# Eight layers on one core: Mamba and the last layer become tasks of the planner that already orders the first six

## The chip, the cores and the metric

The kernel runs on one core of a Trainium2 chip. The time is device microseconds of one execution, from the first to the last instruction and what the device adds around them. Engines: PE multiplies matrices (PEld is its loading of weights), DVE, ACT and POOL work element by element, SP issues the transfers between DRAM and SBUF. PE writes its results to PSUM, which holds eight banks of 512 floats a partition.

## The reference

The input x has 8 sequences of 256 tokens with 128 features, in float32. Eight layers follow each other, and each is used in the same way:

```python
x = x + _layernorm(layer(_layernorm(x)))
```

The layers are a gated delta rule, a block of local attention with a feed-forward part, a line-based attention, a ternary feed-forward network, an attention in tiles, a mixture of experts with two of eight experts, a Mamba pair and a quantized feed-forward network. The change is about the last two. The Mamba layer runs one scan forwards and one over the flipped sequence:

```python
xn = _layernorm(x, ln1_w, ln1_b)
# for each direction m, with E = 256 channels and N = 64 states:
xp, z = split(xn @ W_in.T)
xc = silu(causal_conv4(xp) + conv_b)
dt_lo, Bm, Cm = split(xc @ W_xp.T)           # 8, 64, 64
dt = softplus(dt_lo @ W_dt.T + dt_b);  A = -exp(A_log)
h[t] = exp(dt[t] * A) * h[t-1] + (dt[t] * xc[t]) * Bm[t]     # 256 x 64 values
y[t] = sum_n h[t][:, n] * Cm[t][n] + xc[t] * Dp
out_m = (y * silu(z)) @ W_out.T
# and together:
layer = _layernorm(out_1 + flip(out_2), ln2_w, ln2_b) + xn
```

The last layer is `(silu(x @ wg.T) * (x @ wu.T)) @ wd.T` with 384 hidden features and weights that are integers divided by 127.

## The kernel before

All tokens live in one SBUF tile `k.x`, 16 blocks of 128 tokens. A group g is 4 blocks, 512 tokens, two sequences.

**The first six layers** are written as tasks. A task is a Python generator with a rank (the order in which it was added), a list of tasks that have to be finished before it, and steps divided by `yield`. The class `Turns` is a planner that runs while the program is built: it keeps a clock for each engine, durations for each kind of instruction, and three classes of slots ("ps": four PSUM buffers of two banks each; "4k" and "2k": 25 SBUF buffers of each size). `run` picks the step that can start first, and among equals the one of lowest rank, and emits its instructions. `as_written` then ties each compute engine's queue to the order in which they were emitted, so the engines execute each queue strictly in that order. `S.ps()` hands out a PSUM buffer and writes filler products ahead of a step where the planner expects PE to be idle for over 1.5 us (line 351). A string such as `yield "4k+5"` asks for a slot, and for five more to be free. `change` is a task after the first layer that gives its weights' space to the weights of the last two layers.

**The Mamba layer** stands behind all that, in pools of its own and written out by hand. A unit u is a group and a direction m; there are eight, with 64 states each. `prologue(u)` makes the norms, the convolution, the gate `sz`, the step sizes `dt`, the inputs `dtxT` and the matrices B and C; `epilogue(u)` turns the sum back, adds `D * xc`, multiplies the gate, multiplies by W_out, and for the second direction adds both, takes norms and adds to `k.x`. One state n of a unit is a chain over all engines:

- SP loads one row of C to all partitions (`Cs`, L2046); for even n ACT scales `dtxT` by a column of B (`sT`, L2050); ACT makes `dA` by two exponentials (L2053).
- PE writes the state's input into PSUM: eight transposes of `sT` for even n (L2068), 32 products of 64x64 with the block matrix `dB` for odd n (L2066). POOL makes `dB` for four states at a time (L2040).
- DVE runs the recurrence over 1024 elements (L2074).
- POOL multiplies h by C to `hc` (L2076); for every eighth state DVE does.
- PE adds `hc`, transposed, into the unit's sum `ps_y` in PSUM (L2086).

The loop goes over states: at turn i it writes the inputs of state i-1, starts state i, scans state i-1 and adds state i-4, and then takes one step of the epilogue of the unit before (`behind`) and one of the prologue of the next (`ahead`). PSUM holds three buffers for inputs and everything else and one for `ps_y`.

A layernorm is statistics on DVE (L227, L228), reciprocal roots by powers on POOL (L230, L231), a factor on DVE (L234) and four activations on ACT (L237).

**The last layer** comes behind the Mamba layer: norms of all 16 blocks, and then four blocks of 512 tokens with products for gate and up (L2156, L2157), silu (L2159), product (L2160), the product with wd (L2164) and the norm. Its norms take a square root on ACT (L204), whose table is loaded each time. At last `k.x` is written out (L2221).

Of the kernel before, what the change touches and what calls it, by code (L numbers as in the profile page):

```python
# [17 lines left out]
P = 128  # L18
NB = 8
# [7 lines left out]
UNITS = 4  # L27

# [8 lines left out]
ON_V = 8  # L37

# [134 lines left out]
class Ctx:  # L173
# [46 lines left out]
    def norm_steps(self, dst, src, n):  # L220
# [9 lines left out]
        nc.gpsimd.tensor_scalar(rs, mv[:, :, 1], EPS, None, ALU.add)  # L230
# [54 lines left out]
class Turns:  # L285
# [7 lines left out]
    def __init__(self, k, es, slots):  # L293
        self.nc, self.k = k.nc, k
        self.pools = {
            c: es.enter_context(k.tc.tile_pool(name="turns_" + c, bufs=n, **({"space": PSUM} if c == "ps" else {"side": "right"})))
            for c, n in slots.items()
        }
        self.slots = {c: [0.0] * n for c, n in slots.items()}
        self.clock, self.starts, self.users = {}, {}, {}  # L300
        self.tables = self.mode = None
        self.tiles = {}
        self.tasks = []
        self.now = self.queue = 0.0
        self.filling = False

    def add(self, name, after, steps):
        self.tasks.append((len(self.tasks), list(after), name, steps))
# [15 lines left out]

    def leaving(self, *classes):
        self.leave(*classes)
        return
        yield
# [8 lines left out]
    def adder(self, layer):  # L337
        return lambda name, after, steps: self.add((layer, *name), after, steps)
# [77 lines left out]
    def run(self):  # L416
# [4 lines left out]
        while live or todo:  # L421
            for task in [t for t in todo if all(a in ends for a in t[1])]:
                todo.remove(task)
                order, after, name, steps = task
                live.append([order, max([ends[a] for a in after], default=0.0), {}, name, steps, 0])
            best = None
            for task in live:
                order, ready, needs, _, steps, at = task
                if any(len(self.slots[c]) < n + spare for c, (n, spare) in needs.items()):
# [7 lines left out]
                key = (max(ready, free), order)  # L437
# [1398 lines left out]
def load_l3_attn(k, pool):  # L1836
    k.flip = k.load("c_flip", [P, P], pool)
    k.l3a_ln = k.load("l3a_ln", [P, 4, D], pool, bcast=True)
    k.l3a = []
    for m in ("m1", "m2"):  # L1840
# [3 lines left out]
        k.nc.sync.dma_start(out=w["wdt"][64:73], in_=k.I[f"l3a_{m}_wdt"])  # L1844
        k.l3a.append(w)


def l3_attn(k):

# [12 lines left out]
    N = 64  # L1864
    HALF = (slice(0, 64), slice(64, 128))
    with ExitStack() as es:
        s1 = es.enter_context(k.tc.tile_pool(name="l3a_s1", bufs=1))
        s2 = es.enter_context(k.tc.tile_pool(name="l3a_s2", bufs=2))
        s3 = es.enter_context(k.tc.tile_pool(name="l3a_s3", bufs=3))
        dram = es.enter_context(k.tc.tile_pool(name="l3a_d", bufs=2, space=bass.MemoryType.DRAM))  # L1870
        psum = es.enter_context(k.tc.tile_pool(name="l3a_ps", bufs=3, space=PSUM))
        psumy = es.enter_context(k.tc.tile_pool(name="l3a_psy", bufs=1, space=PSUM))

        def pb(name="ps_a"):
            return psum.tile([P, 2, U], F32, name=name, tag="b")

        for m, w in enumerate(k.l3a):


            w["wk"] = s1.tile([P, 4, 256], F32, name="wk", bufs=2)  # L1880
            cv = s2.tile([P, 4, 256], F32, name="cv", tag="sp_u")
            nc.sync.dma_start(out=cv, in_=k.I[f"l3a_m{m + 1}_conv"].partition_broadcast(P))
            nc.vector.tensor_tensor(w["wk"], cv, over(w["win"][:, 0:256], 4, 1), ALU.mult)
            w["A"] = s1.tile([P, 2, N], F32, name="A", bufs=2)
            nc.scalar.activation(w["A"], w["alog"], AF.Exp)
            nc.vector.tensor_scalar(w["A"], w["A"], 1e-20, -1.0, ALU.max, ALU.mult)
        xTs, CLs = [], []
        for j in range(2):
            t = s1.tile([P, 2, 3 + L], F32, name=f"xT{j}")
            nc.gpsimd.memset(t[:, :, 0:3], 0.0)  # L1890
            xTs.append(t)
            t = s1.tile([P, U], F32, name=f"CL{j}")
            nc.gpsimd.memset(t[64:73, :], 1.0)
            CLs.append(t)
        xns, x1s = {}, {}
        ident64 = k.load("c_ident64", [P, 64], s1)

        def by_seq(t):
            return t.rearrange("p (b t) -> p b t", t=L)

        def turned(name, src):

            t = s2.tile(list(src.shape), F32, name=name)
            for b in range(2):
                for j in range(2):
                    nc.sync.dma_start(out=t[HALF[b], j::2], in_=src[HALF[j], 2 * b:2 * b + 2])
            return t

        def prologue(u, o):
            g, m = divmod(u, 2)  # L1910
            w = k.l3a[m]
            if m == 0:
                xs = xns[g] = s2.tile([P, 4, D], F32, name="xn")
                yield from k.norm_steps(xs, k.x[:, 4 * g:4 * g + 4, :], 4)
                yield from k.norm_steps(xs, xs, 4)
                nc.gpsimd.tensor_tensor(xs, xs, over(k.l3a_ln[:, 0, :], 4, 1), ALU.mult)
                nc.gpsimd.tensor_tensor(xs, xs, over(k.l3a_ln[:, 1, :], 4, 1), ALU.add)
                yield
            xT, CL = xTs[u % 2], CLs[u % 2]
            ps = pb()  # L1920
            for j in range(4):
                d = slice(j * P, (j + 1) * P)
                if m == 0:
                    nc.tensor.transpose(ps[:, 0, d], xns[g][:, j, :], k.ident)
                else:
                    nc.tensor.matmul(ps[:, 0, d], xns[g][:, j ^ 1, :], k.flip, start=True, stop=True)
            yield
            nc.scalar.copy(xT[:, :, 3:3 + L], by_seq(ps[:, 0, :]))
            yield

            xz = s2.tile([P, 4, U], F32, name="xz")
            xc, sz = xz[:, 0:2, :], xz[:, 2:4, :]
            for ec in range(2):
                for b in range(2):
                    ps = pb()
                    for tap in range(4):
                        nc.tensor.matmul(ps[:, 0, 0:L], w["wk"][:, tap, ec * P:(ec + 1) * P], xT[:, b, tap:tap + L], start=tap == 0, stop=tap == 3)
                    yield
                    nc.scalar.activation(xc[:, ec, b * L:(b + 1) * L], ps[:, 0, 0:L], AF.Identity, bias=w["cols"][:, ec, 0:1])
                    yield  # L1940
                    yield
            for ec in range(2):
                ps = pb()
                nc.tensor.matmul(ps[:, 0, :], w["win"][:, 256 + ec * P:256 + (ec + 1) * P], xT[:, :, 3:3 + L], start=True, stop=True)
                yield
                nc.scalar.copy(sz[:, ec, :], ps[:, 0, :])
            yield
            nc.scalar.activation(xz, xz, AF.Silu)
            yield

            ps = pb()
            for ec in range(2):
                nc.tensor.matmul(ps[0:72, 0, :], w["wxp"][:, ec, 64:136], xc[:, ec, :], start=ec == 0, stop=ec == 1)
            for j in range(4):
                for ec in range(2):
                    nc.tensor.matmul(ps[:, 1, j * 64:(j + 1) * 64], xc[:, ec, j * P:(j + 1) * P], w["wxp"][:, ec, 0:64], start=ec == 0, stop=ec == 1)
            yield
            B = s2.tile([P, 4, N], F32, name="B")
            nc.scalar.copy(CL[0:72, :], ps[0:72, 0, :])
            nc.scalar.copy(B.rearrange("p j n -> p (j n)"), ps[:, 1, 0:256])  # L1960
            cd = dram.tile([N, U], F32, name="cd")
            nc.sync.dma_start(out=cd, in_=CL[0:64, :])
            Bt = turned("Bt", B)
            yield
            ps = pb()
            for ec in range(2):
                nc.tensor.matmul(ps[:, ec, :], w["wdt"][64:73, ec * P:(ec + 1) * P], CL[64:73, :], start=True, stop=True)
            dt = s2.tile([P, 2, U], F32, name="dt")
            yield
            nc.scalar.activation(dt, ps, AF.Softplus)  # L1970
            yield
            dtx = s1.tile([P, 2, U], F32, name="dtx")
            nc.gpsimd.tensor_tensor(dtx, dt, xc, ALU.mult)

            nc.gpsimd.memset(dt.rearrange("p e (b t) -> p e b t", t=L)[:, :, :, 0:1], 1e23)
            yield
            yield
            dtxT = s2.tile([P, 4, 2, P], F32, name="dtxT")
            ps = pb()
# [260 lines left out]
```

## Time and profile before

| what | us |
|---|---|
| median of 3 runs | 4137.35 |
| lowest and highest | 4134.76, 4147.18 |
| the profiled execution | 4149.48 |
| its span, first to last instruction | 4147.5 |
| PE, DVE, POOL, ACT busy | 3595.0, 3016.8, 2643.5, 2525.7 |
| first scan of Mamba starts | 2712.3 |
| last scan of Mamba starts | 4059.15 |

A line of the groups gives the code line, engine, operation, what it writes and reads, how often, then busy time and mean duration in ns, then the idle time of the engine ahead of it and what ended most of that. Two rows of the page divide the span into 40 slices and give the busy share of an engine, or the clock granted to PE, in tenths. In a timeline a line is start, duration, engine, code line, operation and tiles, with the idle time ahead of it and its releaser in brackets.

### The profile page before, as it was taken

What the parts mean: (1) busy time and instruction counts of PE and PEld (TensorE: products, weight loads), DVE (VectorE), ACT (ScalarE), POOL (GpSimd) and SP (SyncE); (2) the same over time, 40 slices, a digit from 0 to 9 for tenths busy, and PEclk for the clock granted to TensorE, in tenths of its full rate; (3) what the DMA queues carried; (4) which work ended last, traced back from release to release, by engine and by line L of the source; (5) the groups of instructions that cost most, each with busy time, mean ns of one, the idle gap of its engine ahead of it and who ended that gap; (6) DMA issues with size and microseconds to landing.
All of it is one profiled execution on the core that took longest, in us unless ns stands there. A gap on an engine that the chain in (4) does not pass through costs nothing. (4 is left out here: it accounts for less than half of the span.)

```text
span 4147.5 us, 125166 instructions
## 1 busy us (share of the span) xinstructions
PE 3595.0 (87%) x55265; PEld 2821.2 (68%) x55265; DVE 3016.8 (73%) x4217; ACT 2525.7 (61%) x4465; POOL 2643.5 (64%) x1991
## 2 busy tenths in 40 slices
PE   6989988998888888999899998688988987898886
PEld 4877767777776566655565555377777876777774
DVE  7677677786755666644565568379989987998995
ACT  4555454545444554545354444289979988998993
POOL 5668567666854444331233333479989988998993
PEclk8999999999999999998999898789999999999997
DMA  1000000000001000000000000033323333343430
GB/s 58 3 3 2 3 2 3 3 2 9 2 19 38 1 1 12 25 16 6 1 1 1 6 1 1 11 99 118 111 83 114 109 107 88 110 111 89 118 114 26
DMA packets 98677, 168.89 MB, mean 41 GB/s; under 512 B 16699, under 2 KB 26582, under 8 KB 98006
## 3 DMA queue, kind: packets, MB, share of 16 engines
q1 hardware_dynamic: 98134, 160.89, 13.3%
q8 instruction: 434, 7.11, 0.7%
q14 instruction: 109, 0.89, 0.1%
HBM read 153.51 MB, written 2.10 MB: 38 GB/s over the span
## 5 line engine op out<-in xcount | busy, mean ns | idle before, releaser
L2076 POOL TENSOR_TENSOR hc<-h,Cs 128x1024 f32<-128x1024 f32 x448 | 1049.5, 2372 | 97.1 <-DVE h L2074 85.3
L2074 DVE TENSOR_TENSOR_SCAN h<-dA,ps_h 128x1024 f32<-128x1024 f32 x448 | 988.9, 2266 | 89.8 <-PE ps_h L2068 53.7
L2053 ACT ACTIVATE dA<-dt,A 128x512 f32<-128x512 f32 x1024 | 684.4, 714 | 125.3 <-DVE h L2074 92.6
L2086 PE MATMUL ps_y<-w_c_ident,hc 128*128 128x128 f32 x4096 | 562.1, 281 | 118.7 <-POOL hc L2076 85.3
L2086 PEld LDWEIGHTS ps_y<-w_c_ident,hc 128*128 128x128 f32 x4096 | 454.2, 143 | 173.6 <-POOL hc L2076 158.2
L2050 ACT ACTIVATE sT<-dtxT,B 128x256 f32<-128x256 f32 x1024 | 449.7, 495 | 3.9 <-PE ps_h L2068 3.9
L590 DVE SCALAR_TENSOR_TENSOR acc<-ps,w_l0a_conv,acc 128x254 f32<-128x254 f32 (+2 forms) x768 | 309.5, 471 | 30.6 <-ACT acc L584 30.4
L2066 PE MATMUL ps_h<-dB,dtxTt 64*64 64x64 f32 x16384 | 301.1, 222 | 19.2 <-DVE h L2074 10.1
L2066 PEld LDWEIGHTS ps_h<-dB,dtxTt 64*64 64x64 f32 x16384 | 265.5, 136 | 72.9 <-issue 46.7
L2068 PE MATMUL ps_h<-w_c_ident,sT 128*128 128x128 f32 x2048 | 276.5, 279 | 19.4 <-DVE h L2074 16.9
L2068 PEld LDWEIGHTS ps_h<-w_c_ident,sT 128*128 128x128 f32 x2048 | 239.5, 145 | 31.5 <-DVE h L2074 23.8
L742 POOL TENSOR_TENSOR Ps<-M,w_c_levels 128x512 f32<-128x512 f32 x192 | 241.8, 1274 | 4.8 <-DVE M L716 4.2
L359 ACT COPY XY<-ps 128x1024 f32<-128x1024 f32 (+1 forms) x128 | 120.5, 945 | 179.1 <-PE ps L807 167.1
L230 POOL TENSOR_SCALAR ln_rs<-ln_mv 128x4 f32<-128x4 f32 (+1 forms) x84 | 22.0, 263 | 297.0 <-DVE ln_mv L228 270.5
L800 PE MATMUL ps<-Z,XY 64*64 64x64 f32 x4608 | 172.7, 226 | 35.7 <-DVE Z L784 25.4
L800 PEld LDWEIGHTS ps<-Z,XY 64*64 64x64 f32 x4608 | 144.4, 137 | 53.8 <-DVE Z L784 27.1
L807 PE MATMUL ps<-XY,Z 64*64 64x64 f32 x5120 | 172.0, 224 | 5.2 <-issue 5.1
L784 DVE TENSOR_TENSOR Z<-ps,w_c_ident 128x512 f32<-128x512 f32 x160 | 108.1, 685 | 73.1 <-PE ps L781 71.4
L1633 ACT ACTIVATE e<-ps,nm 128x256 f32<-128x256 f32 x256 | 99.8, 484 | 98.9 <-DVE nm L1630 83.4
L351 PE MATMUL ps<-ident 128*128 128x512 bf16 x401 | 110.0, 426 | 55.2 <-DVE qn L1077 11.5
L2074 DVE TENSOR_TENSOR_SCAN ps_h<-dA,ps_h 128x1024 f32<-128x1024 f32 x64 | 145.6, 2274 | 14.8 <-PE ps_h L2066 14.5
L807 PEld LDWEIGHTS ps<-XY,Z 64*64 64x64 f32 x5120 | 151.1, 138 | 6.9 <-issue 6.9
(451 smaller groups left out, 8572.7 us busy)
## 6 DMA issues: line engine op xcount, KB each, us to landing
Cs<-cd SPq DMA_DIRECT2D x512, 256.0 KB, 3.3
dtxTt<-dtxT SPq DMA_DIRECT2D x32, 128.0 KB, 3.9
wk<-in_l0a_w SPq DMA_DIRECT2D x8, 256.0 KB, 5.7
w_h<-in_l1f_h SPq DMA_DIRECT2D x4, 512.0 KB, 3.9
w_l2a<-in_l2a_w SPq DMA_DIRECT2D x3, 512.0 KB, 4.1
w_l0a_wg<-in_l0a_wg SPq DMA_DIRECT2D x1, 1024.0 KB
w_qk<-in_l0f_wqkv SPq DMA_DIRECT2D x2, 512.0 KB, 3.9
cv<-in_l3a_m_conv SPq DMA_DIRECT2D x2, 512.0 KB, 5.0
```

Of the source, the lines that this page charges most:

```text
L359: self.nc.scalar.copy(out, in_)
L590: nc.vector.scalar_tensor_tensor(acc[:, n, s:L], p4[:, n, 0:L - s], conv[:, h2, 4 * j + n, 3 - s:4 - s], acc[:, n, s:L], ALU.mult, ALU.add,)
L742: nc.gpsimd.tensor_tensor(t, M[:, :, 0:64], over(k.l0a_levels[:, n, :], 8, 1), ALU.mult)
L800: nc.tensor.matmul(ps[own, a, at(j)], XY[rows, t, at(i)], Z[rows, za, at(zj)], start=True, stop=True)
L807: nc.tensor.matmul(ps[to, a, at(4 + j)], Z[rows, za, at(zj)], XY[rows, t, at(i)], start=True, stop=True)
L2050: nc.scalar.mul(st["s"][:, j], o["dtxT"][:, j], o["B"][:, j, n:n + 1])
L2053: nc.scalar.activation(dA[:, :, ec, :], by_seq(o["dt"][:, ec, :]), AF.Exp, scale=w["A"][:, ec, n:n + 1])
L2066: nc.tensor.matmul(ps[q, b, ec, j * 64:(j + 1) * 64], o["dtxTt"][rows, j, ec, q], dB[rows, j, :], start=True, stop=True)
L2068: nc.tensor.transpose(ps[:, j // 2, ec, j % 2 * P:(j % 2 + 1) * P], st["s"][:, j, ec, :], k.ident)
L2074: nc.vector.tensor_tensor_scan(h.rearrange(flat), st["dA"].rearrange(flat), st["in"].rearrange(flat), 0.0, ALU.mult, ALU.add)
L2076: (nc.vector if on_v else nc.gpsimd).tensor_tensor(st["hc"], h, over(by_seq(st["C"]), 2, 2), ALU.mult)
L2086: nc.tensor.matmul(o["py"][:, 2 * b + j, ec, :], st["hc"][:, b, ec, j * P:(j + 1) * P], k.ident, start=first, stop=n == N - 1, is_transpos ...
```

## The change

Mamba and the last layer become tasks of the same planner, so all eight layers share one order, four PSUM buffers and the two classes of SBUF slots.

- Each state of Mamba is a task. It may start when the states eight and nine before it are done (`STATES`). A class of slots "in", without a pool, lets at most two inputs wait in PSUM or be scanned at once. The sum `y` of a unit takes one of the four PSUM buffers; the next unit's is opened when ten states are left.
- The prologue is divided into tasks for the norm, the transposes, the gate and the rest. The gate `sz` and the convolved `xc` are written to DRAM and brought back twelve states before the unit's end (`aside`, `back`). Gate and convolution each have their own silu; the convolution's four parts go into one PSUM buffer.
- The two norms in a row at Mamba's start become one, with a changed epsilon (`twice`).
- The convolution weights folded with W_in and the exponential of `A_log` are made when the weights arrive, during the second layer.
- The last layer is four tasks of 512 tokens, each after the group's second Mamba epilogue. Its norms are those of the planner, without the square root on ACT.
- Tasks may have a rank of their own and a pace that adds to it with each step; Mamba's early tasks leave six slots of each size free while earlier layers still run (`late`, `reserve`).
- `ON_V` is set to 16, but no line uses it any longer: every eighth state still has its product on DVE.

```diff
+STATES, PACE = 8, 1.5
...
-    def norm_steps(self, dst, src, n):
+    def norm_steps(self, dst, src, n, twice=False):
...
+        if twice:
+            nc.gpsimd.tensor_scalar(rs, mv[:, :, 1], 1.0 + EPS, EPS * EPS, ALU.mult, ALU.add)
+        else:
+            nc.gpsimd.tensor_scalar(rs, mv[:, :, 1], EPS, None, ALU.add)
...
+    def more(self, t):
+        self.clock[self.engine] += t
+        self.now = max(self.now, self.clock[self.engine])
...
-                order, ready, needs, _, steps, at = task
-                if any(len(self.slots[c]) < n + spare for c, (n, spare) in needs.items()):
+                order, ready, needs, _, steps, at, pace = task
+                more = self.reserve if order >= self.late > lowest else {}
+                if any(len(self.slots[c]) < n + spare + more.get(c, 0) for c, (n, spare) in needs.items()):
...
-                key = (max(ready, free), order)
+                key = (max(ready, free), order + pace * at)
...
+    def aside(o, name, t):
+        o[name] = k.l3a_dram.tile([P, 2, U], F32, name=name)
+        S.fetch(o[name], t)
+        S.leave("4k")
...
+    def back(u):
+        o = made[u]
+        yield "4k+2 4k"
+        for name in ("xc", "sz"):
+            t = S.tile("4k", [P, 2, U], name)
+            S.fetch(t, o[name])
+            o[name] = t
...
+    def state(u, n):
...
+        on_v = n % 8 == 7
+        yield "2k 4k+1" if n % 2 else "2k 4k+1 4k"
+        C = S.tile("2k", [P, U], "Cs")
...
+        yield "ps in"
+        ps = S.ps().rearrange("p b (e t) -> p b e t", e=2)
...
+        yield "4k" if n % 2 and not on_v else ""
+        h = ps if on_v else S.tile("4k", [P, 2, 2, L], "h")
+        nc.vector.tensor_tensor_scan(h.rearrange(flat), dA.rearrange(flat), ps.rearrange(flat), 0.0, ALU.mult, ALU.add)
+        S.more(1010)
+        if not on_v:
+            S.leave("ps", "in")
+        yield
+        hc = S.tile("4k", [P, 2, 2, L], "hc")
+        (nc.vector if on_v else nc.gpsimd).tensor_tensor(hc, h, over(by_seq(C), 2, 2), ALU.mult)
...
+        add(("r", u), [own("s", u, N - 12), own("z", u)], back(u), rank + N - 12, 1)
+        add(("e", u), [own("r", u)] + [own("s", u, n) for n in range(N)] + [own("e", u - 1)] * m, epilogue(u), rank + N, 2)
+        for n in range(N):
+            i = u * N + n
+            after = [own("s", *divmod(j, N)) for j in (i - STATES, i - STATES - 1) if j >= 0]
...
+            add(("s", u, n), [own("y", u)] + after, state(u, n), rank + n)
...
+    add(("w",), list(soon), weights())
+    for g in H4:
+        add(("f", g), [own("w")] + before(g), forward(g))
...
-            S = Turns(k, es2, {"ps": 4, "4k": N4K, "2k": N2K})
+            S = Turns(k, es2, {"ps": 4, "4k": N4K, "2k": N2K, "in": 2})
...
-            for layer in IN_TURNS:
+            for layer in [l0_attn, l0_ffn, l1_attn, l1_ffn, l2_attn, l2_ffn, l3_attn, l3_ffn]:
...
-        for layer in (l3_attn, l3_ffn):
-            if layer in layers:
-                layer(k)
```

## The prediction

> **What bounds the kernel now.** I read the page first, then the engine table by stretches, then the waits and the timeline at the places that the change touches.
>
> ```profile
> span 4147.5 us, 125166 instructions
> PE 3595.0 (87%) x55265; PEld 2821.2 (68%) x55265; DVE 3016.8 (73%) x4217; ACT 2525.7 (61%) x4465; POOL 2643.5 (64%) x1991
> DVE  7677677786755666644565568379989987998995
> PEclk8999999999999999998999898789999999999997
> ```
>
> PE leads over the span, but the slices disagree: from slice 28 on DVE stands at 8 to 9 with a few 7s, and the slices at either end of that stretch (26 and 40) fall to 3 and 5. The first six layers end near 2660 us, the Mamba layer runs its 512 scans from 2712 to 4061, the last layer takes the rest.
>
> ```profile
> L2076 POOL TENSOR_TENSOR hc<-h,Cs 128x1024 f32<-128x1024 f32 x448 | 1049.5, 2372 | 97.1 <-DVE h L2074 85.3
> L2074 DVE TENSOR_TENSOR_SCAN h<-dA,ps_h 128x1024 f32<-128x1024 f32 x448 | 988.9, 2266 | 89.8 <-PE ps_h L2068 53.7
> 2640.00:2712.00 72.00, 37.31 (x108) 22.34 (x108) 17.12 (x63) 25.04 (x46) 30.64 (x36) 0.64 0.14 42
> 3061.00:3099.00 38.00, 26.47 (x391) 23.36 (x389) 24.38 (x40) 21.96 (x46) 27.16 (x19) 0.87 0.16 53
> 3148.00:3223.00 75.00, 65.57 (x1422) 58.03 (x1424) 74.86 (x37) 68.86 (x130) 73.82 (x37) 1.00 0.40 122
> 4061.00:4147.00 86.00, 49.02 (x212) 32.97 (x210) 35.79 (x143) 28.09 (x43) 16.50 (x14) 0.73 0.04 13
> ```
>
> The last four lines are stretches: length, then busy PE, PE loads, DVE, ACT, POOL. At a steady pace (3148 to 3223) DVE is busy 74.86 of 75 us: 32 scans and 4 multiplications, 18.7 us for eight states. That is the bound. Between two units (3061 to 3099) DVE is busy 24 of 38 us, and ahead of the first scan and behind the last every engine is half idle.
>
> ```profile
> DVE ln_mv L234 <- POOL ln_rs L231: 12.2, 4, 3.7
> DVE ln_st L227 <- POOL x L2028: 4.4, 1, 4.4
> 2636.42 0.19 DVE L1761 TENSOR_TENSOR p<-p,best 128x32 f32<-128x32 f32 x1
> 2712.27 2.29 DVE L2074 TENSOR_TENSOR_SCAN h<-dA,ps_h 128x1024 f32<-128x1024 f32 x1 [35.81 <-PE ps_h L2068]
> 4059.15 2.27 DVE L2074 TENSOR_TENSOR_SCAN ps_h<-dA,ps_h 128x1024 f32<-128x1024 f32 x1
> 4092.02 1.26 POOL L2033 TENSOR_TENSOR x<-x,yn 128x512 f32<-128x512 f32 x1 [2.02 <-DVE ln_st L214]
> 4141.49 0.40 SPq L2221 DMA_DIRECT2D out<-x  x1
> ```
>
> The first two lines are waits of DVE from 3037 to 3126: layernorm steps stand in DVE's queue in front of scans and wait for POOL. The rest mark the last routing of the sixth layer, the first and last scan, the last add of Mamba, the output.
>
> So the time has three parts here: first scan at 2712.3 (P), first to last scan start 1346.9 (W), last scan start to end 88.4 (T).
>
> **P, the start.** In the queues of the changed kernel the first two scans stand on DVE directly behind the subtraction of the last group's routing, which ran at 2636.4. What is added ahead of that place: on PE the first unit's prologue (16 convolution products of 128x256, 2 of the gate, 2 each of the two projections, 16 transposes and small products; by the 0.86 us between 128x512 products about 13 us), on ACT about 16 us (three table switches there and back at 1.28, 1.0 to 2.0 us for each of gate, convolution, softplus and copies), on POOL 2.5 for the norm, 2.3 for dtx, 3.3 for three dB. PE was busy 83 of 100 us from 2500 to 2600, so I let 8 of its 13 us show; ACT was busy 47 of 100 there, its 16 us are covered. The early layers are the same up to the place where the Mamba weights arrive, then reshuffled in the second layer; DVE gains two multiplications of 1.23 for the folded convolution and 0.5 for A, and loses 0.9 for the last layer's weights. Their loads were issued at 1283 to 1291 and first used at 1355, so nobody waits; without that cover it is some 10 us. A reshuffle can cost or win: bounds -10 and +15. P = 2636.4 + 8 + 1 = 2645, from 2630 to 2665.
>
> **W, the scans.** What each engine has to do between first and last scan, counted in the changed queues. DVE: 64 groups of eight at 18.7 are 1197; added are 64 pairs of norm statistics at 0.43 (27.5) and 16 norm factors at 0.16 (2.6), 14 products with D at 0.70 (9.8), 7 copies of y at 1.22 (8.5), 11 half-size evacuations and adds and 9 products of the last layer at 0.69 (13.8), the rest of the sixth layer and two weight conversions (11): 1270. In the kernel before the same count gives 1197 + 31 = 1228 for 1349 to the end of the last scan, so 121 us of DVE were idle. POOL: 448 x 2.33 + 125 x 1.09 + 14 x 2.34 for dtx and gating + 22 x 1.26 + 16 x 1.37 for norms + 10 for the sixth layer's tree = 1273. ACT: 1024 x 0.445 + 1024 x 0.67 = 1142; norms, copies and activations 73; 55 table loads at 1.28 (some 28 before, as gate, convolution and last layer now fall between exponentials) 70: 1285. PE: 512 x (1.10 + 1.09) = 1121 and about 125 for prologues, epilogues and three groups of the last layer. So nothing can go below 1285, and three engines are nearly level.
>
> What becomes of the 121 us? The norm steps that held the scans back stand two to five scans behind their statistics in the new DVE queue, and eight states may be under way, not two or three, so a burst on ACT (a table switch, a 1 us silu, a switch back) eats a reserve. That argues for little idle. Against it, a level load on three engines leaves nowhere to make up a loss, and PSUM gives the scans two buffers, not three. No row shows the new order, so I bound it: no idle gives the 1285 of ACT, all of the old idle 1391. I take 1330, half of the idle, as the steady stretch shows that level engines can run without a gap and the borders show what happens when something stands in front. The gate's and xc's trips through DRAM (32 transfers of 512 KB, 16.8 MB to 161) stand on SP's queue among the Cs loads, where the queue already waits 1004 us on POOL for buffers; DMA is busy 0.40 at most. I cost them at nothing: their cover is the Cs loads' lead, and a late Cs would cost one hc, 2.3 us, at 8 borders.
>
> **T, the end.** From the last scan to Mamba's last add 34.1 us stay. Three of four groups of the last layer move before that. One group: norm 4.7 (4087.2 to 4092.0), transpose and copy 2.0, six products 5.2 warm (0.86 each) or 10.3 cold (1.71), silu and product 1.4, down 2.9 or 5.0, copy 0.6, norm 4.7, add 1.3, output 6.0, hops 0.5: 29 to 37. T = 34.1 + 33 = 67. The rows show both speeds: the first products after 4099 took 1.92, those after 4103 1.02, with the clock at 0.73 in the stretch. The Trainium skill (TensorE: Matmul & The Clock Gate, Part 1) has it that PE needs some 3.4 us of sustained work to get its full clock; by that rule alone the single group would stay cold and T would be 71, and the filler products that the planner puts ahead of it would make it 63.
>
> **Sum.** 2645 + 1330 + 67 = 4042 against 4147.5, -105.5. The profiled run took 4149.5, the median is 4137.4, a ratio of 0.9971: (4042 + 2) x 0.9971 = 4032.
>
> **Rivals.** (1) All of the old idle stays: W 1391, 4093. For it: the borders' waits on PE (50 us) don't come from norms. (2) Slower: the scans starve on PSUM. With two buffers an input may only be written when the scan before the last is over, and DVE needs it 2.2 us later. In the old PE queue one add (1.09) at most stands ahead of each input; in the new one 136 of 512 have two or more, 165 adds too many. An add, an input and 0.2 of hops are 2.39, level with 2.34; with two adds 3.48, 1.1 late. 165 x 1.09 = 180: W 1510, 4212. It decides from W = 1440 on, 0.33 us a state. Against it: elsewhere 170 inputs have no add ahead. The Trainium skill (Perfetto Trace Analysis, Optimization Strategy) says that gaps which repeat on the engine that should be full can mean too little PSUM for the next tile; no run here shows it with two buffers. (3) The sum of the busiest engine holds: W 1285, 3987. (4) The order doesn't do what it says, the last layer or the first scans end up outside Mamba: 9 of 12 silu products stand ahead of the last scan in the queue, so hardly.
>
> **Numbers.** Forecast (W 1290 to 1380) 0.56, idle stays 0.14, starved 0.20, engine sum 0.08, not as said 0.02. Low end: 2630 + 1285 + 63 gives 3968. High end: idle stays with P 2665 and T 71 gives 4117; part of the starved cases brings it to 4140. What a measurement can tell from no change is about 0.3%, 4125 to 4150. Faster: 0.56 + 0.14 + 0.08 = 0.78. Of the 0.22 left, starved or not as said, 0.04 stops within that band and 0.18 goes beyond it.
>
> **What would show it.** First scan near 2645, some 65 us earlier; eight states at 18.7 in mid unit and no stretch above 30 at the borders; DVE's waits for POOL's norms gone; one group of the last layer behind the last scan, 67 us to the end. Wrong if scans wait for PE all through a unit, if POOL or ACT falls behind (18.7 becoming 20), or if the second layer, near 1350 to 1700 us, is longer.

## The result: 4190.6 us, slower by 1.35%

The changed kernel takes 4190.55 us (median of 4 runs, 4184.46 to 4191.68) against 4136.06 of the kernel before in the same comparison: ratio 1.0135, 95% interval 1.0117 to 1.0153. The forecast was 4032, its range ended at 4140. The profiled execution has a span of 4188.9, 41.4 more than before, and divides as follows:

| us | P, to first scan | W, first to last scan | T, last scan to end |
|---|---|---|---|
| before | 2712.3 | 1346.9 | 88.3 |
| forecast | 2645 | 1330 | 67 |
| after | 2652.4 | 1475.3 | 61.2 |

P and T came out as forecast and brought 87 us. W took 128 and is the whole error: 145 over its forecast. The profiled execution of the kernel before was 13 us above its median, so the medians are 54.5 apart and not 41.4, and the table is likely to put P's gain too high (the last section has the numbers). The page after:

```profile
span 4188.9 us, 125746 instructions
PE 3615.2 (86%) x55450; PEld 2833.4 (68%) x55450; DVE 3032.6 (72%) x4152; ACT 2507.6 (60%) x4458; POOL 2649.6 (63%) x1999
DVE  7677676776765666645674667689889898898895
PEclk8999999999999899999998989999999999999999
L2080 POOL TENSOR_TENSOR hc<-h,Cs 128x1024 f32<-128x1024 f32 x448 | 1051.3, 2372 | 198.1 <-DVE h L2074 138.2
L2074 DVE TENSOR_TENSOR_SCAN h<-dA,ps 128x1024 f32<-128x1024 f32 x448 | 996.8, 2270 | 141.0 <-PE ps L2068 65.6
```

The hole that DVE had between the sixth layer and Mamba (the 3 in slice 26 before) is a 6 now, and the last slice is still a 5. But of the twelve slices from 28 to 39 eight stood at 9 before, and five do now, and the idle time in front of scans (behind the second bar of the last line) rose from 89.8 to 141.0, most of it for PE. Of the 89.8, 35.8 stood ahead of the first scan, outside W; within W, with the scans that write to PSUM counted too, the idle time went from 69 to 153. The duration of a scan is the same. By stretches, with the same columns as before (length, then busy PE, loads, DVE, ACT, POOL, clock, DMA share, GB/s): the first unit, which took 161 us before; a steady stretch of 32 states; the end.

```profile
2652.00:2841.00 189.00, 158.07 (x2849) 134.01 (x2848) 165.03 (x108) 156.43 (x296) 159.49 (x88) 0.95 0.33 105
3685.00:3762.00 77.00, 63.70 (x1350) 57.40 (x1348) 74.09 (x35) 69.92 (x134) 73.35 (x36) 1.00 0.50 155
4130.00:4188.00 58.00, 38.82 (x194) 21.35 (x194) 12.94 (x44) 11.85 (x23) 14.24 (x15) 0.94 0.07 19
```

In the steady stretch DVE is no longer full: 74.09 of 77, some 19.2 us for eight states where it was 18.7. Over all of W the sums of the engines were near the forecast except one: DVE 1288 (forecast 1270), POOL 1263 (1273), PE 1236 (1246), ACT 1194 (1285, too high by 91). So no engine became the bound by its work. Of W's 128 us, 62 are work that moved into it (DVE was busy 1226 us there before) and 66 are idle time of DVE, which grew from 121 to 187. Of the 145 over the forecast, 18 are work and 127 idle time. The waits in that stretch say where it stood (us in total, times, longest), first in the kernel before, where the first line still holds the 35.8 ahead of the first scan, then after:

```profile
DVE h L2074 <- PE ps_h L2068: 53.7, 17, 35.8
DVE h L2074 <- PE ps_h L2066: 17.9, 15, 3.2
DVE ln_mv L234 <- POOL ln_rs L231: 30.4, 10, 3.7
PE ps_y L2086 <- POOL hc L2076: 82.9, 138, 1.5
```

```profile
DVE h L2074 <- PE ps L2068: 65.6, 35, 13.9
DVE h L2074 <- PE ps L2066: 51.5, 46, 4.5
DVE ln_mv L238 <- POOL ln_rs L235: 9.4, 4, 3.3
PE ps L2092 <- POOL hc L2080: 146.4, 158, 3.2
```

DVE's waits for POOL's norm steps (`ln_mv`) fell from 30.4 to 9.4; with those of the statistics that wait for POOL's `x`, from 43.7 to 16.6. In their place scans wait for PE's inputs, and PE itself stands at an add (L2092) that waits for POOL's product. Before, adds waited 82.9 for POOL too, but rarely with a late scan close behind. Of the scans that were late for PE, 7 had such a wait in the 4.5 us in front of them before, with at most 5 us of idle time between them; after it is 38, with at most 26. A place before, where an add waits and the scans go on without a gap (DVE scans from 3169 to 3184):

```profile
3179.70 1.09 PE L2086 MATMUL ps_y<-w_c_ident,hc 128*128 128x128 f32 x8 [1.37 <-POOL hc L2076]
3180.72 1.16 PE L2066 MATMUL ps_h<-dB,dtxTt 64*64 64x64 f32 x64
```

One such place after, from the timelines of PE and then DVE (start, duration, engine, what, idle ahead of it):

```profile
3699.18 1.09 PE L2068 MATMUL ps<-w_c_ident,sT 128*128 128x128 f32 x8
3700.11 1.04 PE L2092 MATMUL ps<-w_c_ident,hc 128*128 128x128 f32 x8
3703.95 1.96 PE L2092 MATMUL ps<-w_c_ident,hc 128*128 128x128 f32 x16 [2.81 <-POOL hc L2080]
3705.84 1.16 PE L2066 MATMUL ps<-dB,dtxTt 64*64 64x64 f32 x64
3707.14 6.64 DVE L2074 TENSOR_TENSOR_SCAN h<-dA,ps 128x1024 f32<-128x1024 f32 x3 [0.43 <-PE ps L2066]
```

Two adds (x16) stand in front of an input. The first waits 2.81 us for POOL, the input behind it comes late, and so does the scan. I counted for each input how many scans back the nearest add in front of it on PE belongs to. Before it is the fourth scan back for 508 of 512 (the first four have none). After it is the third or nearer (a near input, below) for some 200 of 512 (203 in the count of the expectations below), and those had 124 of the 153 us that DVE was idle ahead of scans. With the rows' durations, a scan 2.27, its product 2.37, an add 1.09, an input 1.09 and 0.3 of hops make a ring of 7.1 us. Three scans back leave it 6.6 to 6.8. But a ring that is too long by 0.3 to 0.5 makes small gaps, and 69 of the 124 us stand in 19 gaps of over 2 us. So the count marks where the time is lost; it does not show alone that the ring loses it.

### The profile page after: what moved, and what is told of

Its sections match the earlier page's. It is cut to its first block, busy times and chain, and to the rows that moved or that the text cites. A ratio compares the mean times of both kernels' runs of the same rounds, so it can differ in the third digit from the quotient of the medians.

```text
span 4188.9 us, 125746 instructions
## 1 busy us (share of the span) xinstructions
PE 3615.2 (86%) x55450; PEld 2833.4 (68%) x55450; DVE 3032.6 (72%) x4152; ACT 2507.6 (60%) x4458; POOL 2649.6 (63%) x1999
## 5 line engine op out<-in xcount | busy, mean ns | idle before, releaser
L2074 DVE TENSOR_TENSOR_SCAN h<-dA,ps 128x1024 f32<-128x1024 f32 x448 | 996.8, 2270 | 141.0 <-PE ps L2068 65.6
L2055 ACT ACTIVATE dA<-dt,w_l3a_m_alog 128x512 f32<-128x512 f32 x1024 | 660.2, 710 | 63.6 <-POOL hc L2080 40.3
L2092 PE MATMUL ps<-w_c_ident,hc 128*128 128x128 f32 x4096 | 543.1, 280 | 157.9 <-POOL hc L2080 148.8
L2092 PEld LDWEIGHTS ps<-w_c_ident,hc 128*128 128x128 f32 x4096 | 456.2, 143 | 215.8 <-POOL hc L2080 191.9
L2066 PE MATMUL ps<-dB,dtxTt 64*64 64x64 f32 x16384 | 298.3, 224 | 21.6 <-DVE h L2074 14.3
L2066 PEld LDWEIGHTS ps<-dB,dtxTt 64*64 64x64 f32 x16384 | 267.1, 138 | 66.5 <-issue 32.5
L2068 PE MATMUL ps<-w_c_ident,sT 128*128 128x128 f32 x2048 | 275.9, 280 | 35.0 <-DVE h L2074 30.0
L2068 PEld LDWEIGHTS ps<-w_c_ident,sT 128*128 128x128 f32 x2048 | 233.6, 144 | 56.5 <-issue 17.1
L362 PE MATMUL ps<-ident 128*128 128x512 bf16 x586 | 157.5, 419 | 84.8 <-ACT e L1645 19.2
L362 PEld LDWEIGHTS <-ident 128*128 128x128 bf16 x586 | 61.1, 105 | 159.0 <-issue 91.5
L2074 DVE TENSOR_TENSOR_SCAN ps<-dA,ps 128x1024 f32<-128x1024 f32 x64 | 145.6, 2276 | 12.4 <-PE ps L2066 8.3
```

The costliest lines, as they stand in the source:

```text
L362: self.nc.tensor.matmul(ps[:, 0, :], self.k.ident16, over(self.k.ident16, 4, 1), start=True, stop=True)
L2055: nc.scalar.activation(dA[:, :, ec, :], by_seq(o["dt"][:, ec, :]), AF.Exp, scale=w["A"][:, ec, n:n + 1])
L2066: nc.tensor.matmul(ps[q, b, ec, j * 64:(j + 1) * 64], o["dtxTt"][rows, j, ec, q], o["dB", n // 4][rows, n % 4 // 2, j, :], start=True, sto ...
L2068: nc.tensor.transpose(ps[:, j // 2, ec, j % 2 * P:(j % 2 + 1) * P], sT[:, j, ec, :], k.ident)
L2074: nc.vector.tensor_tensor_scan(h.rearrange(flat), dA.rearrange(flat), ps.rearrange(flat), 0.0, ALU.mult, ALU.add)
L2092: nc.tensor.matmul(o["y"][:, 2 * b + j, ec, :], hc[:, b, ec, j * P:(j + 1) * P], k.ident, start=o["added"] == 1 and j == ec == 0, stop=o[" ...
```

## The experiments

W, P and T below come from the profiled execution of each run, times are medians. All kernels are the changed one with the edit shown, except where the kernel before is named. Each edit makes the planner write another order for more than the instructions that it names, so that a difference of W is not always the named cause alone.

**e1, three inputs in PSUM.**

```diff
-            S = Turns(k, es2, {"ps": 4, "4k": N4K, "2k": N2K, "in": 2})
+            S = Turns(k, es2, {"ps": 4, "4k": N4K, "2k": N2K, "in": 3})
```

> One number is changed in the changed kernel: three inputs may wait in PSUM or be scanned at once, where two could. The planner writes another order for it: of the 512 inputs on PE, the nearest add ahead belongs to a scan three or fewer before for 108 where it is 203 in the changed kernel. Theory PSUM (two buffers starve the scans): most of the 129 us that the stretch from first to last scan lost go, W (1476 in the changed kernel) falls to 1345 to 1390 and the time to 4060 to 4105. Theory ORDER (an add that the planner puts close in front of an input ties the scan to POOL's product of a scan just before): the ring gets looser for half of the near inputs only, W falls by 30 to 70, time 4120 to 4160. Theory GATES (transfers in SP's queue hold back the Cs loads): nothing changes, 4180 to 4200.

Measured: 4180.6 us (ratio to before 1.0107, 1.0087 to 1.0126), W 1459.3. By PSUM most of the 128 us should have come back, and 16 did, so two inputs are not the cause. ORDER's forecast of 4120 to 4160 failed too: near inputs fell to about half and the adds' waits for POOL from 146.4 to 83.0, as in the kernel before, yet the near inputs left still have 112 of 139 us idle ahead of scans. How many there are does not set the loss. The time fits GATES, which e3 tests.

**e2, adds written later.** After POOL's product in `state`:

```diff
             S.more(400)
+        S.now += 4400
```

> The changed kernel with two inputs in PSUM as it is; only the planner is told that POOL's product is done 4.4 us later than it thinks, so that it writes the adds into PE's queue further back: the nearest add ahead of an input belongs to a scan three or fewer before for 99 of 512 inputs instead of 203 rows, and to one five or more before for 366. Theory ORDER: the scans no longer wait for adds; the 147 us that adds waited on POOL at the head of PE's queue fall below 80, W falls by 50 to 100, time 4090 to 4140. Theory PSUM: two buffers are still two buffers, W within 20 of the changed kernel, time 4170 to 4210.

Measured: 4136.9 us (0.9999, 0.9987 to 1.0010), W 1415.0, with the two PSUM buffers as they were. In the order that ran, the third scan back or nearer stands in front of 32 inputs, not 99 as expected. PE's waits now, in the same stretch:

```profile
PE ps L2068 <- DVE h L2074: 51.3, 63, 1.7
PE ps L2066 <- DVE h L2074: 20.1, 33, 1.0
PE ps L2093 <- POOL hc L2080: 8.7, 18, 1.6
```

Adds wait 8.7 for POOL instead of 146.4. PE waits for DVE to free PSUM more than in the changed kernel, and in mid-unit that costs nothing, as DVE is then the one that is full: 24 of the 63 stretches of eight states take 18.8 us or less, where it was 4 in the changed kernel and 31 before. One line that moves adds back in PE's queue gives 54 us of the time back. Of the 60 us of W, 42 are idle time of DVE; the other 18 are work of DVE that the new order has outside W or on ACT (six of the seven copies of y, 1.2 us each, among it). The line also lets each state's task end later for the planner, and so others start later; that was not taken apart.

**e3, gate and xc stay in SBUF.** `aside` is left out, `back` loads nothing.

> The changed kernel, but the gate and the convolved xc stay in SBUF until the unit's end: none of the 32 transfers of 512 KB to DRAM and back is left. Theory GATES: SP's queue no longer stands behind ACT's gate (68 and 193 us of its waits), Cs loads come earlier, POOL's products too; W falls by 50 or more, time below 4140. Theories PSUM and ORDER: the Cs loads were early enough (POOL waited 4 us for them in the changed kernel), so nothing is won but what a changed order of the planner gives either way; the time stays within 20 of the changed kernel, 4170 to 4210.

Measured: 4203.4 us (1.0159, 1.0139 to 1.0179), W 1493.1. Without the 32 transfers nothing is won, so GATES falls. It is 13 us slower, with another order written by the planner.

**e4, only the states in the old order.** A task for each turn of the old loop; prologue, gate, epilogue and last layer stay the planner's.

> The states of Mamba in the turn order of the kernel before (inputs of state i-1, start of i, scan of i-1, add of i-4, one task for each turn), but everything else of the change kept: one planner, queues tied to the written order, first unit's prologue within the sixth layer, last layer by groups within Mamba, gates in DRAM. On PE the nearest add ahead of an input belongs to the fourth scan before for 509 of 512. Theory ORDER: W returns to that of the kernel before, 1347, less up to 44 of norm waits and plus up to 40 for the added work of the last layer, 1305 to 1390; with P 2650 and T 65 the time is 4020 to 4105. Theory GATES, or a theory that the last layer's work within Mamba is what costs: W stays above 1440, time above 4155.

Measured: 4292.2 us (1.0368, 1.0343 to 1.0394), W 1570.7, a clear miss of ORDER as I had put it. Adds are four scans back for 508 inputs, 14 of the 63 stretches of eight take 18.8 us or less, and yet 12 are longer than 30 us (6 after, 3 before). Adds at their old distance are not enough: in this order the loss stands between the states. The edit also writes no filler products while states are under way (so do e5, e6, e10, e11 and e16), and the granted clock over W was 0.93 instead of 0.98; what that costs was not separated.

**e5 and e6, the whole old loop as a chain of tasks**, one step of the epilogue and one of the prologue a turn; e6 with three groups of the last layer as steps too.

```diff
+        if g in FWD:
+            yield
+            yield from S.forward(g)
...
+        for side in ("behind", "ahead") if i < 8 * N + 3 else ("ahead",):
+            next(sides[side], None)
```

> The loop of the kernel before, whole (each turn: inputs of state i-1, start of i, scan of i-1, add of i-4, one step of the epilogue behind, one of the prologue ahead), as one chain of tasks of the planner, its queues tied to the written order. Kept from the change: first unit's prologue within the sixth layer, one norm for two, the folded weights in the second layer, the planner's norms in the last layer. Taken back: the gate's trip to DRAM, the last layer by groups (all four groups stand behind Mamba), the planner's places for prologue and epilogue. Theory PLACES (what the planner puts between the states, and where, is what W lost beyond the adds): W 1310 to 1350 as in the kernel before, P 2650 to 2670, T 80 to 88, time 4045 to 4100. Theory QUEUES (to tie Mamba's queues to the written order costs by itself, a scheduler of the compiler had mended it before): W above 1400, time above 4140.

> The same with the last layer's first three groups as further steps of the epilogue behind, one for each turn, so that one group is left at the end. It adds 9 products on DVE (6 us), 9 silu with their table loads on ACT (some 30 us), 18 products of 128x512 on PE and three pairs of norms to W. If the last layer is hidden in Mamba: W rises by 10 to 25 over the run without it, T falls to 60 to 67, time 4035 to 4090, the same or lower. If ACT has no room for it: W rises by 40 or more and the time is above the run without it by 20.

Measured: e5 4175.4 us (1.0110, 1.0089 to 1.0131), P 2633.1, W 1440.1, T 97.5. e6 4178.5 (1.0120), W 1474.7, T 66.3. PLACES had forecast 4045 to 4100, which failed; QUEUES' bound held. Between the two the last layer within Mamba costs 34.6 on W and saves 31.2 on T: nothing is won. And the early start is no clean gain: in e5 the first unit takes 197.7 us, and pieces of the sixth layer stand among scans of the third unit:

```profile
3079.26 0.29 DVE L1826 TENSOR_TENSOR y<-ps,ye 128x128 f32<-128x128 f32 x1 [7.41 <-POOL ye L1824]
3087.99 0.29 DVE L1826 TENSOR_TENSOR y<-ps,ye 128x128 f32<-128x128 f32 x1 [6.25 <-POOL ye L1824]
```

**e7, the kernel before with Mamba's queues tied.**

```diff
-                layer(k)
+                with as_written(tc, COMPUTE):
+                    layer(k)
```

> The kernel before; only its Mamba layer's queues are tied to the written order, as the changed kernel's are. Theory QUEUES: 4160 or more. Theory PLACES: within 20 of the kernel before, 4115 to 4150, as its written order is already one state a turn.

Measured: 4196.1 us against 4130.1 (1.0167, 1.0139 to 1.0196), W 1389.1, T 98.9. Part of what I had read as a gain of the changed kernel, norms that no longer hold DVE's queue, is here alone: the wait of `ln_mv`, 30.4 us before, is gone (that for POOL's `x` stays, 15.2), and the kernel is 66 us slower. PE's queue shows what came instead (tied, then the untied kernel before, in the stretch of its scans):

```profile
PE ps_a L2009 <- POOL t L2003: 29.2, 7, 4.5
PE ps_a L1983 <- POOL dtx L1973: 18.6, 7, 3.0
PE ps_a L1924 <- POOL xn L1917: 17.8, 3, 5.9
```

```profile
PE ps_a L1983 <- POOL dtx L1973: 1.6, 4, 0.4
```

In the written order PE stands at products of the epilogue and the prologue until POOL has made their input, with the states' inputs behind. In the kernel before the compiler's scheduler had put such steps elsewhere; the changed kernel takes that freedom away.

**e8, later adds and three inputs.**

> Later adds (4.4 us more for POOL's product in the planner) and three inputs instead of two. The nearest add ahead belongs to a scan three or fewer before for 27 of 512 inputs. If two buffers still starve the scans once the adds are out of the way: 15 to 40 below the run with later adds alone (4137), 4095 to 4125. If PSUM is no limit: within 12 of it, 4125 to 4150.

Measured: 4151.2 us (1.0055, 1.0037 to 1.0073), W 1437.0, just above the range for PSUM as no limit. With adds out of the way a third buffer wins nothing.

**e9 to e12, the last two layers not tied**: the changed kernel, e5, e6 and e2, with this in `as_written`, where `loose` holds the two layers' instructions:

```diff
-        if ins.engine in engines:
+        if ins.engine in engines and ins.name not in loose:
```

> The changed kernel, all of it, but the instructions of its last two layers are no longer tied to the written order: the planner still writes them, and the compiler's scheduler may move one in front of another that waits, as it could in the Mamba layer of the kernel before. The first six layers stay tied. Distances of adds stay near: 228 inputs have an add of the third scan before or nearer ahead of them (203 rows in the changed kernel). Theory QUEUES (tying costs about what it cost the kernel before, 60): 4115 to 4150. Theory ORDER (the planner's order costs by itself, and the scheduler keeps most of it): 4170 to 4200.

> The old loop as a chain of tasks (e5), its last two layers no longer tied. Distances: fourth scan before for 484 of 512, as in the kernel before. Theory QUEUES: W returns to 1340 to 1360 and T to 88 to 95, P stays at 2635 to 2655, time 4070 to 4110, below the kernel before. Otherwise 4150 to 4180 as with the tie.

> The same with three groups of the last layer as steps within Mamba (e6), not tied. Theory QUEUES: 4065 to 4110. If the last layer within Mamba costs what it saves, within 12 of the run without it.

> Later adds (e2, 4137) and the last two layers not tied: the nearest add belongs to a scan three or fewer before for 53 of 512 inputs. If late adds and loose queues are two costs that add up: 4075 to 4110. If they are one cost seen twice (loose queues only let inputs pass adds): 4125 to 4145.

Measured: e9 4263.8 us (1.0303, 1.0274 to 1.0332), 73 slower than tied; e10 4162.6 (1.0068), 13 faster than e5; e11 4175.9 (1.0093), as e6; e12 4167.9 (1.0077), 31 slower than e2. Only e10, in its "otherwise", came out within a stated range. So to tie is not bad by itself. The old loop gains a little by freedom (the intervals of e5 and e10 overlap), the planner's order loses by it: in e9 adds wait still longer for POOL,

```profile
PE ps L2096 <- POOL hc L2084: 196.6, 174, 10.1
```

and QUEUES fails as a cause of the changed kernel's loss. What the compiler's scheduler goes by was not looked at.

**e13 and e15, the first scan behind the sixth layer**, with the changed kernel and with e2:

```diff
-        add(("y", u), [own("p", u)] + [own("s", u - 1, N - 10)] * (u > 0), opened(u))
+        add(("y", u), [own("p", u)] + ([own("s", u - 1, N - 10)] if u else before(3)), opened(u))
```

> The changed kernel, but the first unit's sum is opened, and so its first scan starts, only when the sixth layer is done; its prologue stays early. In the changed kernel the first scan started at 2652 and the first unit took 189 us, with the rest of the sixth layer between its scans. Theory PAID BACK (what an early first scan wins is lost again in the first unit): P rises by 25 to 45, the first unit falls to 150 to 165, the time stays within 15 of the changed kernel, 4175 to 4205. Theory CLEAN GAIN: the first unit stays above 180 and the time rises by the whole of P, 4215 to 4240.

> Later adds (e2, 4137) and the first scan behind the sixth layer. By PAID BACK within 15 of 4137; by CLEAN GAIN 4165 to 4180.

Measured: e13 4175.3 us (1.0104, 1.0081 to 1.0127), P 2679.0, first unit 164.3 instead of 188.7, W 1431.3. Of the 27 us that P loses, the first unit alone gives 24 back. The other 20 that W fell come from later units, some shorter and some longer, which a later start doesn't explain. e15: 4164.9 (1.0061, 1.0039 to 1.0082), P 2693.4, W 1407.9: with late adds the first unit gives 22 back, W as a whole only 7, and the early start is worth some 28. In the profiled run 14 of that are no effect of the edit, as P is that much above e13's with the same order up to the first scan. So PAID BACK holds in the changed kernel and not with e2.

**e14, the last layer behind Mamba.**

```diff
-        add(("f", g), [own("w")] + before(g), forward(g))
+        add(("f", g), [own("w")] + before(3), forward(g))
```

> The changed kernel, but all four groups of the last layer stand behind the last unit of Mamba, as in the kernel before. Theory PAID BACK (three groups within Mamba cost there what they save at the end; with the old loop e6 against e5 it was 35 on W for 31 on T): W falls by 25 to 40, T rises by 25 to 35, time 4178 to 4202. Theory HIDDEN: W falls by less than 15, time 4205 to 4220.

Measured: 4173.7 us (1.0083, 1.0054 to 1.0113), W 1421.8, T 85.7. Units one to four are within 2 us of the changed kernel's; the last four fall from 750 to 696. The order of instructions is the changed kernel's until the fifth unit has begun, so this is the cleanest of the edits. Three groups of the last layer cost W 53.5, 25 in DVE's work and 29 in its idle time, and save 24.5 of T; for W both theories had expected less.

**e16, the old loop, not tied, first scan behind the sixth layer.**

> The old loop, not tied (e10, 4163), with the first scan behind the sixth layer: in e5 and e10 pieces of the sixth layer ran as late as 3090, between scans that waited 7 and 6 us for them. PAID BACK: P 2660 to 2690, first unit 160 to 168 instead of 205, W 1350 to 1385, T 90 to 95, time 4110 to 4150, below e10. CLEAN GAIN: 4190 or more.

Measured: 4162.6 us (1.0066, 1.0045 to 1.0087), P 2680.8, W 1390.5, T 94.1. First unit 172.6 instead of 204.8; of the 50 us that P loses W gives 37 back, and the time is that of e10, in neither forecast. Why the old loop is still 44 longer on W within the planner than in the kernel before stays open.

**e17 and e18, later adds and the last layer behind Mamba; e18 also writes the prologue's steps later:**

```diff
-                task[1], task[2] = self.now, {}
+                task[1], task[2] = self.now + self.slack(task[3]), {}
```

> Later adds (e2) and the last layer behind Mamba (e14) together; the early first scan stays. In e14 W fell by 53 and T rose by 25; P there was 17 longer with the same order of instructions up to the first scan. If the two costs add up: W 1365 to 1390, T 84 to 88, time 4100 to 4125, below the kernel before. If they are one cost (PE overfull in the last units either way): 4130 to 4150.

> The same, and the planner takes each step of a prologue or a gate for ready 1.5 us later than it thinks, so that it writes it further behind what it waits for: silu of the convolution then stands less often at the head of ACT's queue while PE is still at the convolution (in e2, 2916 to 2938: ACT idle 3.4, DVE 8.3 us). If this head of the queue is what is left at the borders: the stretches of eight states above 30 us (e2 had 8) become fewer than 4, W falls by 10 to 40 below e17, 4070 to 4110. If not: within 12 of e17.

Measured: e17 4145.5 us (1.0029, 1.0017 to 1.0042), W 1400.3, T 86.0. e18 4137.5 (1.0009, 0.9993 to 1.0025), W 1391.7, T 89.3, with four stretches of eight above 30 us in both. The two costs don't add up: 60 and 53 of W alone, 75 together, and as T rises by 21 against e2, e17 is 9 us slower than e2. The heads of ACT's queue that e18 moves are not what is left at the borders; its edit also leaves out the filler products ahead of these steps. No version beat the kernel before; e2 and e18 come level with it.

## Why the prediction was wrong

**What bounds the kernel: right.** DVE at 18.7 us for eight states is the bound in mid-unit, and e2 returns to it.

**P: right in its number, in part by luck.** 2652.4 for 2645. The sum took the routing's subtraction at 2636.4 and let 9 us follow it; the subtraction ran at 2651.6, and the first scan 0.9 behind it. With the same order up to the first scan, P was 2669.6 in e14, beyond the forecast's 2665 (the last section). And the step stopped too early: it counted 11 us of DVE work for the rest of the sixth layer that moves into W, and the first unit took 27 us more than before. e13 shows that of it: 24 of 27 us.

**T: right.** 61.2 for 67, a single group behind the last scan. Its first products took 1.98 for two of them, the next 3.45 for four, 0.86 each, with filler products between and the clock at 0.94. The Trainium skill (TensorE: Matmul & The Clock Gate, Part 1) has the array at full speed after some 3.4 us of sustained work; this trace agrees as far as it goes (fillers for 12.25 us, and 0.86 from the first product on; it does not measure the 3.4), and by its rule the fillers' value of 63 was the right one of my two.

**W: the step that failed.** I took "1330, half of the idle", from bounds of 1285 and 1391. That is 1270 of DVE's work and 60 of idle time; they measured 1288 and 187. The lower bound was ACT's sum, which measured 1194 and not 1285 (its exponentials and multiplications are 660 + 434 = 1094 us by their rows, not 1142, and all the rest 100, not 143). The upper bound, "all of the old idle", was no bound: idle grew by 66. Two reasons given for little idle were wrong. Eight states under way were to be a reserve, but a scan can't start before its input, and that stands on PE behind adds that wait for POOL (146.4 us), however many states have begun; e2 moves these adds and idle falls by 42. And the freed norm waits were to be a gain; most of them did go, and e7 shows that the strict order which removes them costs the kernel before 66 us.

**What took W's 128 us.** Taken away alone, adds close in front of inputs give 60 back (e2: 18 work, 42 idle), the last layer within Mamba 53 (e14: 25 work, 29 idle), the early first scan 44 (e13: 18 work, 26 idle), of which only the first unit's 24 are plainly its own. They overlap: the first two together give 75 (e17), and the early start gives 7 once adds are late (e15). So they are not a sum, and the 53 us of W by which e17 is still longer than the kernel before stay open.

**Rival 2 was near.** It had W 1510 and 4212, with the right place, adds in front of inputs on PE, and a chance of 0.20. Its price was wrong, though W came near it (1475): it charged each add too many with PE's 1.09, 165 of them. In e2's order 171 are too many, and W is 60 shorter; what differs there is that they no longer stand at the head of the queue and wait for POOL. Its condition, two PSUM buffers, was wrong: e1 and e8. There the Trainium skill (Perfetto Trace Analysis, Optimization Strategy) had said that repeating gaps can mean too little PSUM; here they did not, the measurement decides. Rivals 1, 3 and 4 fell.

**Transfers of the gate: right**, at nothing that shows. POOL waited 4.1 us for Cs, and e3 is no faster.

## What to carry to other kernels

When an order is kept by queues, look for each step at what stands at the head of each queue and which engine it waits for: a consumer written right behind its producer's planned end holds everything behind it, and writing it one or two periods later cost nothing in mid-unit here (e2). Work that fills a hole elsewhere is won only if the stretch into which it moves has a hole too; price it there by the bounding engine and by the queue that it heads, not by its busy time. An idle sum of the old order is no upper bound for a new one.

## What the runs showed of the hardware

The same order of instructions gives a different P. Up to the first scan the queues of e14 are those of the changed kernel, but it starts at 2669.6 instead of 2652.4. The granted clock between 1500 and 2000 us was 0.94 instead of 0.97 (the last three numbers are clock, DMA share and GB/s; the changed kernel first, then e14), and the 17 us had gathered before 2060, 6 to 9 of them before 1200:

```profile
1500.00:2000.00 500.00, 459.14 (x3639) 300.90 (x3638) 280.10 (x541) 263.82 (x492) 177.10 (x207) 0.97 0.04 12
1500.00:2000.00 500.00, 457.59 (x3595) 299.40 (x3593) 284.83 (x546) 259.92 (x487) 185.44 (x210) 0.94 0.04 12
```

The kernel before and e7 have one order through the first six layers as well. The last routing's subtraction ran at 2636.4 in the one and at 2614.3 in the other, with 0.94 and 0.97 in the same stretch. A difference of 15 to 22 us in P between two profiled runs need not be the kernel's. That is why the shares above are read from W and T.
